# Two chained cross attentions on one core: memsets on VectorE, added attention, output sums and first FFN sums at other steps, and another order of the first attention's head groups

## The chip, the cores and the metric

The kernel runs on one core of one Trainium2 chip. The metric is the device time of one execution in microseconds. Engines are named as the profile does: PE is TensorE (matmuls and transposes), PEld its weight loads, DVE is VectorE, ACT is ScalarE, POOL is GpSimd, SP is SyncE, which here only issues DMAs.

## The reference

`x` and `ctx` have 32 items of 256 tokens by 256 features, all in float32. Two layers follow each other.

```python
# L0: 16 heads of 16 features
q, k, v = x @ Wq.T, ctx @ Wk.T, ctx @ Wv.T
att = softmax(q k^T / sqrt(16)) v
x = x + att[0]                     # item 0's attention is added to every item

# L1
nX = layernorm(ctx) * n1w + n1b
nF = layernorm(x) * n2w + n2b
attended = softmax(nF nX^T / 16) nX
h = gelu(attended @ fc1.T + fc1_b)             # 256 -> 4
cross = h @ fc2.T + fc2_b                      # 4 -> 256
nC = layernorm(cross) * n3w + n3b
self = softmax(nC nC^T / 16) nC
out = nF + gamma2 * (cross + gamma1 * self)
```

Since only `att[0]` is used, L0 is computed for item 0 alone. Since `h` has 4 columns, everything behind the first attention of L1 is done with rows of 5 or 6 numbers per token.

## The kernel before, in words

`x` stays in SBUF as `x_all` (128 partitions, 32 items, 2 halves of the tokens, 256 features). `ctx` comes in quarters of four items (`cq`). Every engine runs its instructions in the order in which the program issues them; nothing is reordered, so the order of the Python calls is the schedule.

**L0 (about 5 to 35 us).** The 16 heads are four groups (the fours) `j = 0..3`. For each, `head_queries(j)` makes the scores by queries (`sq`), `head_maxima` takes the negated maxima on VectorE (L493), `head_less(j)` turns them on TensorE (`pm`) and adds them into `qmT` on VectorE (L505), `head_keys(j)` makes the scores by keys (`sk`) and their exponentials on ScalarE (L514), `head_values(j)` multiplies them with the values (`ph`) and copies the result (L375, on ScalarE or VectorE), `head_turned(j)` turns it (`pt_h`), and its `weighted()` divides by the sums on VectorE (L534, L535). In between stand other works: `stats(n)` takes the statistics of items of `ctx` (VectorE, L211, two instructions an item), `moments_c` and `moments_ahead` make mean and scale of them (GpSimd, one power of some 1.65 us among them, L227), `even_normed` and `odd_normed` normalise token halves on GpSimd and ScalarE, and `setup_bias()` makes a row by a small product `p_b1f` with an addition on VectorE (L589). The PSUM banks of tag `tp` are two, and shared by nearly all of these.

**Cross attention (about 36 to 174 us).** `first_step(s)` runs for s = 0 to 34; scores exist for s = 0 to 31. In a step TensorE turns the exponentials of item s - 2 (`pt_e`), `x` of item s + 1 (`pt_x`), `ctx` of item s + 4 (`pt_c`), then multiplies the scores of item s (`sc`, L786). Each quarter has two more products (`pf` at b == 1, `pv` at b == 2, where b = s % 4). VectorE takes statistics of item s + 12 of `ctx` and s + 8 of `x` (L211), copies `pt_c` to `nxT` (L352), then takes the negated maximum `nm` of the scores (L796). ScalarE copies `pt_x` to `nfT` with a scale and a bias (L768) and makes the exponentials `e` (L799). GpSimd normalises `x` (L333) and `ctx` (L307), and at the end of a quarter makes the moments of the next one (`moments_both`, with a power of 2.93 us on 16 columns).

Works that belong to no single item are put at steps by hand:

- `add_attention(lo, hi)` (L758) is a DMA issued from GpSimd that adds `att` to items of `x_all` in SBUF. It must land before `stats_x` of these items.
- `zeroed`, eight memsets (L927) of the tiles `v_sl`, `u_sl`, `t_sl` at steps 8 to 15: six of 128x1024, then two of 128x64 and 128x128.
- The tables `between` (calls inside a step, just ahead of its scores) and `beside` (calls after the step). `hide(0, 4)` divides the first half of the FFN's inputs and adds the bias (a reciprocal, a product and a sum on VectorE, L1000, L1006, L1008). `activate(0)` is the gelu of them on ScalarE, with a table load (L1009). `third_a` to `third_d` are the third norm, by turns on GpSimd (`w_m`, `vgv`, `r` with a power, `w_k`) and VectorE.
- `output_gammas` and `output_bias` multiply and add rows of 5x256 on VectorE (L653, L654, L657, L658), `output_rows` does two more (L661, L662) and then issues eight small DMAs on SP's queue into `w_out`, which the output products read from 179 us on.

**Self attention and output (about 172 to 223 us).** An order written out word by word (`order`), TensorE always ahead.

Of the kernel before, what the change touches and what calls it, by code (L numbers as in the profile page):

```python
# [22 lines left out]
QB = 4  # L23
# [4 lines left out]
def tile_xattn_seq(  # L28
# [33 lines left out]
    nc = tc.nc  # L62
    B = x.shape[0]
    NQ = B // QB
    NT = B * NC
    TQ = QB * NC
    NM, NK = FH + 1, FH + 2
# [366 lines left out]
    def project_values(t, copy):  # L434
        pp = bank("tp", f"pp_v{t}")
        for dc in range(NC):
            nc.tensor.matmul(
                pp[:, t, :],
                c0T[:, dc, t * P : (t + 1) * P],
                wvT[:, dc, :],  # L440
                start=(dc == 0),
                stop=(dc == NC - 1),
            )
        copy(v1[:, t, :, 0:DK], pp[:, t, :].rearrange("p (h e) -> p h e", e=DK))
# [39 lines left out]
    def head_queries(j):  # L484

        sq = four_banks(f"sq{j}")
        qk = qT[:, j, :], kT[:, j, :]
        pair_products((0, *qk, sq[0:2]), (1, *qk, sq[2:4]))
        return sq

    def head_maxima(j, sq, heads):
        for i in heads:
            nc.vector.tensor_reduce(  # L493
                m_all[:, j % 2, :, i, ones_at[j % 2]], sq[i], AX.X, ALU.max, negate=True
            )
# [11 lines left out]
    def head_keys(j):  # L507

        sk = four_banks(f"sk{j}")
        kq = kT[:, j, :], qmT[:, j % 2, :]  # L510
        pair_products((0, *kq, sk[0:2]), (1, *kq, sk[2:4]))
        eT_of[j] = wk.tile([P, QB, NC, D], F32, tag="eTq", name=f"eT_h{j}", bufs=2)
        for i in range(QB):
            nc.scalar.activation(eT_of[j][:, i], sk[i], AF.Exp)  # L514
# [4 lines left out]
    def head_values(j, copy=nc.scalar.copy, by_pairs=False):  # L519
        col_of[j] = by_columns(  # L520
            tp_bank,
            f"h{j}",
            lambda kt, i: v1[:, kt, head_of(j, i), :],
            eT_of.pop(j),
            copy,
            by_pairs,
        )
# [55 lines left out]
    def setup_bias():  # L583
        pb = bank("tp", "p_b1f")
        for dc in range(NC):
            nc.tensor.matmul(
                pb[:, 0, 0:FH], ones, b1f[:, dc, :], start=(dc == 0), stop=(dc == NC - 1)
            )
        nc.vector.tensor_add(fc1b_all, pb[:, 0, 0:FH], fc1b_bc)  # L589
# [59 lines left out]
    w_out = const.tile([P, D], F32)  # L649
    nc.gpsimd.memset(w_out, 0.0)  # L650

    def output_gammas():
        nc.vector.tensor_mul(g1r, g1r, g2r)  # L653
        nc.vector.tensor_mul(g2r, g2r, m5)  # L654

    def output_bias():
        nc.vector.tensor_mul(tail, tail, g1r)  # L657
        nc.vector.tensor_add(g2r, g2r, tail)  # L658

    def output_rows():  # L660
        nc.vector.tensor_add(g2r, g2r, bias2)  # L661
        nc.vector.tensor_mul(g1r, g1r, k6[0:NM, :])  # L662
        for j in range(QB):
            nc.sync.dma_start(w_out[SL * j : SL * j + NM, :], g2r)
            nc.sync.dma_start(w_out[SL * j + NM : SL * j + 2 * NM, :], g1r)
# [6 lines left out]
    def stats(*ns):  # L672
        for n in ns:
            stats_c(n)
# [22 lines left out]
    head_less(1)()  # L697
    setup_outer()
    stats(3)
    project_values(1, on_scalar)  # L700
    moments_c(0)
    even_normed(0, 1, 2, 3)
    sq = head_queries(2)
    stats(4)
    head_maxima(2, sq, (0, 1))
    head_values(0)
    setup_bias()
    head_maxima(2, sq, (2, 3))
    head_keys(1)
    odd_normed(0, 1)  # L710
    weighted = head_turned(0)
    stats(5)
    head_less(2)()
    weighted()
    sq = head_queries(3)
    stats(6)
    head_maxima(3, sq, range(QB))
    head_values(1)
    odd_normed(2, 3)
    head_keys(2)  # L720
    weighted = head_turned(1)
    stats(7)
    moments_c(1)
    even_normed(4, 5)
    head_less(3)()
    weighted()
    head_keys(3)
    stats(8, 9, 10)
    head_values(2, by_vector)
    stats(11)  # L730
    odd_normed(4)
    head_values(3, on_scalar, True)
    c_ends = moments_ahead(2)
    weighted = head_turned(2), head_turned(3)
    for f in weighted:
# [140 lines left out]
    def first_step(s, between=()):  # L876
        q, b = s // QB, s % QB
        if b == 0 and 2 <= q and q + 4 < NQ:
            load_c(q + 4)
            if q == 2:  # L880
                load_x((NQ - 2) * QB, B)
        if s == QB:
            add_attention(QB * QB, (QB + 1) * QB)
        elif b == 0 and 1 < q < NQ - 3:
            add_attention((q + 3) * QB, (q + 4) * QB)

        late_turn = s in (27, 29, 31)
        if 0 <= s - 2 < B and not late_turn:
            cross_turned(s - 2)
        if 2 <= s < 2 * QB:  # L890
            for n in (2 * s, 2 * s + 1):
                stats_x(n)
            if s < QB:
                ends = first_moments(2 * s, 2 * s + 2)
        if QB <= s and s + 3 * QB < B:
            stats_c(s + 3 * QB)
        if s >= 2 * QB and s + 2 * QB < B:
            stats_x(s + 2 * QB)
        if b == QB - 1 and 4 <= q + 2 < NQ:
            if q + 3 < NQ:  # L900
                moments_both(q + 2)
            else:
                moments_x(q + 2, 0, QB)
        if QB < s < B - 1:
            turn_x(s + 1)
        for n in {9: (12,), 10: (13, 14), 11: (15,)}.get(s, ()):
            even_x(n)
        if 3 * QB <= s < B - 2 * QB:
            even_x(s + QB)

        for n in {10: (12, 13), 11: (14, 15), 12: (), 13: (16, 17), 16: (), 17: (20, 21)}.get(
            s, (s + QB,) if 3 * QB <= s < B - 2 * QB else ()
        ):
            odd_x(n)
        if B - 2 * QB < s <= B - QB:
            norm_x(s + QB - 1)
        if s + QB < B and s >= QB:
            turn_c(s + QB, on_scalar if s < QB + 2 else by_vector)
        for n in {7: (13,), 8: (14, 15), 9: (16, 17), 10: (18,)}.get(s, ()):
            norm_c(n)  # L920
        if 2 * QB + 2 < s < B - 2 * QB:
            norm_c(s + 2 * QB)
        for n, at in enumerate(scaled_at):
            if s == at:
                scale_skip(n)
        if 2 * QB <= s < 2 * QB + len(zeroed):
            nc.gpsimd.memset(*zeroed[s - 2 * QB])  # L927
        if b == 2 and 1 < q < NQ:
            values_turned(q)
        if b == 1 and 1 < q < NQ:  # L930
            values(q)
        if b == 2 and 0 < q <= NQ:
            cross_values(q - 1)
        if b == 3 and 0 < q <= NQ:
            cross_weighted(q - 1)
        for f, *args in between:
            f(*args)
        if s < B:
            softmax = cross_scores(s)
            if s <= QB:  # L940
                turn_x(s + 1)
            if s == 0:
                turn_c(6, nc.scalar.copy)
            softmax()
        if late_turn:
            cross_turned(s - 2, by_vector if s == B - 1 else on_scalar)
        if 1 <= s <= QB:
            stats_c(s + 3 * QB - 1)
        if s == 0:
            first_ends.pop()()  # L950
            add_attention(3 * QB, 4 * QB)
            add_first(3)
            first_ends.append(first_moments(3, QB))
            odd_normed(7)
        elif s == 1:
            first_ends.pop()()
            odd_normed(8)
            even_normed(8, 9)
        elif s == 2:
            ends()  # L960
            turn_c(7)
            load_c(5)
            odd_normed(9)
            even_normed(10)
        elif s == 3:
            ends()
            values(1)
            even_normed(11)
        elif s == QB:
            values_turned(1)  # L970
        if s in (QB, QB + 1):
            odd_normed(s + 6)
        if s == QB:
            moments_x(2, 0, 2)
        elif s == QB + 1:
            norm_x(2 * QB)
            moments_x(2, 2, QB)
        elif s == QB + 2:
            norm_x(2 * QB + 1)
            moments_c(3)  # L980
            norm_x(2 * QB + 2)
            norm_c(3 * QB)
        elif s == QB + 3:
            norm_x(2 * QB + 3)
        elif s == 2 * QB:
            moments_both(3)
# [179 lines left out]
    def activate(lo):  # L1166
        gelu_of.pop(lo)()

    between = {
        20: [(hide, 0, 4)],  # L1170
        28: [(turn_t, 0, by_vector)],
        29: [(turn_u, 2, by_vector), (early_weights, 0), (hide, 4, 6)],
        30: [(activate, 4), (third_a, 2), (turn_t, 1, by_vector)],
        31: [(third_c, 2), (self_values, 0)],
    }
    beside = {
        20: [(activate, 0), (third_a, 0)],
        21: [(third_b, 0), (third_a, 1)],
        22: [(third_c, 0), (third_b, 1)],
        23: [(output_gammas,), (output_bias,)],  # L1180
        24: [(third_d, 0), (output_rows,)],
        25: [(third_c, 1), (turn_u, 0, by_vector)],
        26: [(turn_u, 1, by_vector), (early_scores, 0), (third_d, 1)],
        28: [(early_scores, 1)],
# [197 lines left out]
```

## Time and profile before

| | us |
|---|---|
| time, median of 3 runs (226.4 to 227.15) | 226.84 |
| the profiled execution's own time | 226.24 |
| its span in the profile | 224.5 |
| TensorE busy in the span | 207.7 |
| VectorE busy | 170.2 |
| ScalarE busy | 146.5 |
| GpSimd busy | 174.3 |
| granted TensorE clock, mean | 0.989 |

The profile is of one execution. Its span runs from the first to the last instruction; the execution's own time is 1.7 us more. In a timeline row stand the start, the duration, the engine, the line, the operation, the tiles written and read, their shapes, how many instructions were merged, and in brackets the idle time of the engine before it with what ended it. Matmuls overlap, so a row's duration is longer than the distance to the next row; a pause of TensorE is seen in the starts. The step of a row is found by counting the scores: those of steps 8 to 16 start at 71.19, 75.32, 79.78, 83.14, 86.43, 90.56, 95.44, 98.80 and 101.84 us, those of steps 20 to 25 at 117.38, 122.13, 127.55, 130.91, 133.95 and 139.06.

### The profile page before, as it was taken

How to read it: one execution, taken by the hardware profiler on the slowest of the kernel's cores; microseconds unless marked ns; L12 is line 12 of the kernel's file. 1: busy time of each engine (PE TensorE's matmuls, PEld its weight loads, DVE VectorE, ACT ScalarE, POOL GpSimd, SP SyncE). 2: the span in 40 equal slices, each digit the busy share in tenths (PEclk: the TensorE clock that was granted, in tenths of full speed). 3: DMA queues.
4: the chain of work that ended last, by engine and by line, in shares of the span. 5: the costliest groups of instructions: out<-in, count | busy, mean ns of one | idle time of the engine just before them, and what ended most of it. 6: DMA issues, size and time to landing. Idle time of an engine off the chain costs nothing.

```text
span 224.5 us, 4955 instructions
## 1 busy us (share of the span) xinstructions
PE 207.7 (93%) x1797; PEld 152.7 (68%) x1797; DVE 170.2 (76%) x408; ACT 146.5 (65%) x300; POOL 174.3 (78%) x276
## 2 busy tenths in 40 slices
PE   7999988899999999999999898999999999999960
PEld 6666547576777888697796696787757566665640
DVE  2787989899988777758668579486548699978791
ACT  2454877698979488766766986548594684545510
POOL 6056588586889999999999889999229978999700
PEclk9999999999999999999999999999999999999995
DMA  7699998999976995082280000000000031542787
GB/s 212 218 334 352 391 385 226 177 260 244 247 131 242 306 200 189 1 141 49 38 153 0 1 3 1 6 3 0 3 1 0 3 142 48 219 158 93 274 311 262
DMA packets 18054, 33.81 MB, mean 151 GB/s; under 512 B 1191, under 2 KB 2158, under 8 KB 18030
## 3 DMA queue, kind: packets, MB, share of 16 engines
q1 hardware_dynamic: 12990, 24.33, 30.2%
q0 software_dynamic: 3696, 7.34, 18.9%
q10 hardware_dynamic: 1344, 1.84, 2.4%
q8 instruction: 14, 0.23, 0.4%
q14 instruction: 10, 0.08, 0.1%
HBM read 17.73 MB, written 8.39 MB: 116 GB/s over the span
## 4 chain that ended last, share of the span: by engine, by line
PE 43%; POOL 23%; DVE 16%; DMA 8%; ACT 4%; issue 3%; DVEq 0%; ACTq 0%; SPq 0%; POOLq 0%
PE sc L786 7%; POOL cq L307 6%; DVE st L211 5%; PE o L452 4%; DMA x_all<-att 4%; POOL rs_b L227 4%; PE k L452 4%; PE pu L364 4%; PE q L452 2%; PE sc L452 2%; POOL x_all L333 2%; DMA wk_nat<-in_L_xattn_Wk_dram 2%; DVE nm L796 2%; DMA fc_nat<-in_L_xattn_fc_w_dram 2%; PE ph L364 2%
## 5 line engine op out<-in xcount | busy, mean ns | idle before, releaser
L786 PE MATMUL sc<-nxT,nfT 128*128 128x256 f32 x256 | 62.4, 386 | 0.7 <-ACT nfT L768 0.7
L786 PEld LDWEIGHTS sc<-nxT,nfT 128*128 128x128 f32 x256 | 45.7, 190 | 12.1 <-issue 5.3
L799 ACT ACTIVATE e<-sc,nm 128x256 f32<-128x256 f32 x64 | 26.9, 472 | 26.1 <-DVE nm L796 25.8
L777 POOL TENSOR_TENSOR x_all<-x_all,w_bc 128x512 f32<-128x512 f32 x32 | 39.8, 1270 | 0.0
L796 DVE TENSOR_REDUCE nm<-sc 128x2 f32<-128x512 f32 x32 | 22.0, 688 | 23.2 <-PE sc L786 11.0
L768 ACT ACTIVATE nfT<-pt_x,bq,wq 128x256 f32<-128x256 f32 x64 | 33.2, 579 | 1.6 <-PE pt_x L202 1.5
L211 DVE BATCH_NORM_STATS2 st<-x_all 128x6 f32<-128x256 f32 x64 | 23.2, 412 | 2.6 <-DMA x_all<-att 2.5
L202 PE MATMUL pt_x<-ident,x_all 128*128 128x128 f32 x132 | 20.6, 277 | 2.9 <-POOL x_all L333 1.1
L202 PE MATMUL pt_c<-ident,cq 128*128 128x128 f32 x132 | 19.6, 275 | 1.4 <-ACT nfT L768 1.0
L211 DVE BATCH_NORM_STATS2 st<-cq 128x6 f32<-128x256 f32 x56 | 20.6, 412 | 0.0
L1225 DVE TENSOR_TENSOR x_all<-o,x_all 128x1024 f32<-128x1024 f32 (+1 forms) x19 | 18.1, 993 | 2.9 <-PE o L452 2.4
L1220 ACT ACTIVATE eT<-k 128x512 f32<-128x512 f32 (+1 forms) x19 | 14.3, 798 | 9.1 <-PE k L452 7.8
L202 PEld LDWEIGHTS pt_x<-ident,x_all 128*128 128x128 f32 x132 | 15.0, 141 | 6.9 <-POOL x_all L333 2.7
L307 POOL TENSOR_SCALAR cq<-cq,rs_b,nmr_b 128x256 f32<-128x256 f32 x32 | 19.4, 677 | 0.0
L202 PE MATMUL pt_e<-ident,e 128*128 128x128 f32 x128 | 19.1, 274 | 0.0
L808 ACT COPY eTq<-pt_e 128x512 f32<-128x512 f32 x31 | 17.9, 584 | 0.2 <-PE pt_e L202 0.2
L202 PEld LDWEIGHTS pt_e<-ident,e 128*128 128x128 f32 x128 | 15.6, 141 | 3.0 <-issue 0.4
L202 PEld LDWEIGHTS pt_c<-ident,cq 128*128 128x128 f32 x132 | 15.1, 141 | 2.6 <-ACT nfT L768 1.4
L352 DVE COPY nxT<-pt_c 128x512 f32<-128x512 f32 x23 | 15.5, 675 | 0.7 <-PE pt_c L202 0.7
L452 PE MATMUL o<-w_out,vt 32*128 32x256 f32 x128 | 13.3, 400 | 0.6 <-ACT vt L1101 0.5
L452 PE MATMUL k<-tt,ut 32*128 32x256 f32 x112 | 13.6, 397 | 0.0
L1207 DVE TENSOR_REDUCE t_sl<-q 128x4 f32<-128x1024 f32 (+1 forms) x12 | 12.3, 1041 | 0.3 <-PE q L452 0.2
(224 smaller groups left out, 433.3 us busy)
## 6 DMA issues: line engine op xcount, KB each, us to landing
out_dram<-x_all SPq DMA_DIRECT2D x15, 512.0 KB
x_all<-att POOLq DMA_DIRECT2D x7, 1024.0 KB, 9.2
cq<-in_ctx_dram SPq DMA_DIRECT2D x6, 1024.0 KB
x_all<-in_x_dram SPq DMA_DIRECT2D x4, 1024.0 KB
x_all<-in_x_dram SPq DMA_DIRECT2D x1, 2048.0 KB
x_all<-in_x_dram SPq DMA_DIRECT2D x1, 1792.0 KB
cq<-in_ctx_dram ACTq DMA_DIRECT2D x1, 1024.0 KB
cq<-in_ctx_dram SPq DMA_DIRECT2D x1, 768.0 KB
```

Of the source, the lines that this page charges most:

```text
L202: nc.tensor.transpose(pt[:, dc, t * P : (t + 1) * P], src[:, t, dc * P : (dc + 1) * P], ident)
L211: nc.vector.bn_stats(st[:, t, :], src[:, t, :])
L307: nc.gpsimd.tensor_scalar(row, row, rs[:, i + t, :], nmr[:, i + t, :], ALU.mult, ALU.add)
L352: copy(nxT_of[q][:, b], pt)
L452: nc.tensor.matmul(dst[i][:, t, :], lhs[r : r + SL, t * P : (t + 1) * P], rhs[r : r + SL, :], start=True, stop=True,)
L768: nc.scalar.activation(nfT_of[n][:, dc, :], px[:, dc, :], AF.Identity, bias=bq[:, dc : dc + 1], scale=wq2[:, dc : dc + 1],)
L777: nc.gpsimd.tensor_mul(x_all[:, n], x_all[:, n], w2_bc.unsqueeze(1).to_broadcast([P, NC, D]))
L786: nc.tensor.matmul(sc[:, qt, :], nfT[:, dc, qt * P : (qt + 1) * P], nxT[:, dc, :], start=(dc == 0), stop=(dc == NC - 1),)
L796: nc.vector.tensor_reduce(nm, sc, AX.X, ALU.max, negate=True)
L799: nc.scalar.activation(e[:, qt, :], sc[:, qt, :], AF.Exp, bias=nm[:, qt : qt + 1])
L808: copy(eT_of[q][:, b], turned(e_of.pop(n), "et", f"e_{n}"))
L1225: nc.vector.tensor_add(xs, po, xs)
```

## The change

In L0, the order of the calls after `stats(3)` is another one: `setup_bias`, the third group's queries and `stats(4)` come first, the four maxima of the third group stand together, the first group's values follow the second group's keys, the first group's weighting follows the last `head_less`, and the second group's `head_turned` follows the last keys. The third group's copy (L375) moves from VectorE to ScalarE. The added attention of items 24 to 27 goes from step 12 to step 11, that of items 28 to 31 from step 16 to step 15. The eight memsets go from GpSimd to VectorE, behind the maximum of their step. `hide(0, 4)` goes from the inside of step 20 to the end of step 19. The six output sums, in steps 23 and 24 before, are put one by one at the ends of steps 16, 17, 18, 21, 22 and 23, and the eight small DMAs follow the last one.

```diff
-    def output_gammas():
-        nc.vector.tensor_mul(g1r, g1r, g2r)
-        nc.vector.tensor_mul(g2r, g2r, m5)
-
-    def output_bias():
-        nc.vector.tensor_mul(tail, tail, g1r)
-        nc.vector.tensor_add(g2r, g2r, tail)
+    output_sums = [
+        lambda: nc.vector.tensor_mul(g1r, g1r, g2r),
+        lambda: nc.vector.tensor_mul(g2r, g2r, m5),
+        lambda: nc.vector.tensor_mul(tail, tail, g1r),
+        lambda: nc.vector.tensor_add(g2r, g2r, tail),
+        lambda: nc.vector.tensor_add(g2r, g2r, bias2),
+        lambda: nc.vector.tensor_mul(g1r, g1r, k6[0:NM, :]),
+    ]
 
     def output_rows():
-        nc.vector.tensor_add(g2r, g2r, bias2)
-        nc.vector.tensor_mul(g1r, g1r, k6[0:NM, :])
         for j in range(QB):
...
     stats(3)
+    setup_bias()
+    sq = head_queries(2)
+    stats(4)
     project_values(1, on_scalar)
     moments_c(0)
     even_normed(0, 1, 2, 3)
-    sq = head_queries(2)
-    stats(4)
-    head_maxima(2, sq, (0, 1))
+    head_maxima(2, sq, range(QB))
+    head_keys(1)
+    head_less(2)()
     head_values(0)
-    setup_bias()
-    head_maxima(2, sq, (2, 3))
-    head_keys(1)
+    stats(5, 6)
+    sq = head_queries(3)
     odd_normed(0, 1)
     weighted = head_turned(0)
-    stats(5)
-    head_less(2)()
-    weighted()
-    sq = head_queries(3)
-    stats(6)
     head_maxima(3, sq, range(QB))
     head_values(1)
     odd_normed(2, 3)
     head_keys(2)
-    weighted = head_turned(1)
+    head_less(3)()
     stats(7)
     moments_c(1)
     even_normed(4, 5)
-    head_less(3)()
     weighted()
     head_keys(3)
+    weighted = head_turned(1)
+    weighted()
+    head_values(2)
     stats(8, 9, 10)
-    head_values(2, by_vector)
+    head_values(3, on_scalar, True)
     stats(11)
     odd_normed(4)
-    head_values(3, on_scalar, True)
     c_ends = moments_ahead(2)
...
         if s == QB:
             add_attention(QB * QB, (QB + 1) * QB)
-        elif b == 0 and 1 < q < NQ - 3:
-            add_attention((q + 3) * QB, (q + 4) * QB)
+        elif s == 2 * QB:
+            add_attention((QB + 1) * QB, (QB + 2) * QB)
+        elif b == QB - 1 and 1 < q < QB:
+            add_attention((q + 4) * QB, (q + 5) * QB)
...
-        if 2 * QB <= s < 2 * QB + len(zeroed):
-            nc.gpsimd.memset(*zeroed[s - 2 * QB])
...
             softmax()
+        if 2 * QB <= s < 2 * QB + len(zeroed):
+            nc.vector.memset(*zeroed[s - 2 * QB])
...
     between = {
-        20: [(hide, 0, 4)],
...
     beside = {
+        16: [(output_sums[0],)],
+        17: [(output_sums[1],)],
+        18: [(output_sums[2],)],
+        19: [(hide, 0, 4)],
         20: [(activate, 0), (third_a, 0)],
-        21: [(third_b, 0), (third_a, 1)],
-        22: [(third_c, 0), (third_b, 1)],
-        23: [(output_gammas,), (output_bias,)],
-        24: [(third_d, 0), (output_rows,)],
+        21: [(third_b, 0), (third_a, 1), (output_sums[3],)],
+        22: [(third_c, 0), (third_b, 1), (output_sums[4],)],
+        23: [(output_sums[5],), (output_rows,)],
+        24: [(third_d, 0)],
```

## The prediction

> **What bounds the kernel now.** I read the page first, then TensorE's timeline through the cross attention, then the timelines of VectorE and GpSimd around each place where TensorE paused. On the page TensorE is busy nearly throughout, and GpSimd is full in slices 14 to 24 of the 40.
>
> ```profile
> PE 207.7 (93%) x1797; PEld 152.7 (68%) x1797; DVE 170.2 (76%) x408; ACT 146.5 (65%) x300; POOL 174.3 (78%) x276
> POOL 6056588586889999999999889999229978999700
> ```
>
> A busy share hides short pauses, so I measured TensorE's cadence in its timeline. Four transposes are followed by the next group 0.43 to 0.44 us later (88.16 to 88.59). Anything beyond that is a wait. The pairs below show five of them:
>
> ```profile
> 88.16 0.60 PE L202 MATMUL pt_e<-ident,e 128*128 128x128 f32 x4
> 88.59 0.60 PE L202 MATMUL pt_x<-ident,x_all 128*128 128x128 f32 x4
> 92.39 0.60 PE L202 MATMUL pt_e<-ident,e 128*128 128x128 f32 x4
> 93.20 0.66 PE L202 MATMUL pt_x<-ident,x_all 128*128 128x128 f32 x4 [0.21 <-POOL x_all L333]
> ...
> 103.57 0.60 PE L202 MATMUL pt_e<-ident,e 128*128 128x128 f32 x4
> 104.54 0.63 PE L202 MATMUL pt_x<-ident,x_all 128*128 128x128 f32 x4 [0.36 <-DVE nxT L352]
> ...
> 119.11 0.60 PE L202 MATMUL pt_e<-ident,e 128*128 128x128 f32 x4
> 120.13 0.63 PE L202 MATMUL pt_x<-ident,x_all 128*128 128x128 f32 x4 [0.42 <-DVE nxT L352]
> ...
> 125.75 0.66 PE L202 MATMUL pt_c<-ident,cq 128*128 128x128 f32 x4 [0.75 <-ACT nfT L768]
> ...
> 137.06 0.63 PE L202 MATMUL pt_x<-ident,x_all 128*128 128x128 f32 x4 [0.78 <-POOL sq_x L224]
> ```
>
> Start minus start minus 0.44 gives 0.37, 0.53, 0.58, then 0.92 at 125.75 (the group before began at 124.40) and 0.95 at 137.06 (before: 135.68). A sixth, 0.19, stands at 85.50. Together: 3.54 us. VectorE shows why for three of them:
>
> ```profile
> 103.05 0.75 DVE L211 BATCH_NORM_STATS2 st<-x_all 128x6 f32<-128x256 f32 x2 [0.91 <-DMA x_all<-att]
> 103.72 0.68 DVE L352 COPY nxT<-pt_c 128x512 f32<-128x512 f32 x1
> ...
> 118.64 0.75 DVE L211 BATCH_NORM_STATS2 st<-x_all 128x6 f32<-128x256 f32 x2 [1.62 <-DMA x_all<-att]
> ...
> 134.87 1.44 DVE L658 TENSOR_TENSOR g2r<-g2r,tail 5x256 f32<-5x256 f32 x1
> 136.24 0.67 DVE L352 COPY nxT<-pt_c 128x512 f32<-128x512 f32 x1
> ```
>
> TensorE's next x transposes start 0.15 behind the end of the copy nxT (104.40 to 104.54), and that copy stood behind statistics that waited for an added attention, or (at 137.06, whatever name the row gives) behind the output sums. GpSimd shows where the late transfers were issued:
>
> ```profile
> 94.16 0.95 POOL L927 MEMSET u_sl<- 128x1024 f32 x1
> 95.06 1.27 POOL L758 DMA_DIRECT2D x_all<-att  x1
> ...
> 134.64 1.40 POOL L1023 TENSOR_TENSOR w_k<-u_sl,gram_k 128x576 f32<-128x576 f32 x1
> ```
>
> **Added attention for items 24 to 31.** Issued in steps 11 and 15, no longer 12 and 16. In GpSimd's queue step 11 begins at 87.91 and step 15 at 102.65, against issues at 95.06 and 109.31. So both leave about 7 us sooner, and the 8 to 9 us to landing (95.06 to 103.0) then end before steps 16 and 20 read them. Each issue, 0.90 to the next start, now stands ahead of the combined moments of its step (4.7 us) and the norms behind them; the memsets gone from the same queue pay for that. x of 24 to 31 must have landed: its queue moved its last bytes by 82, GpSimd comes at about 85. Gain 0.53 + 0.58.
>
> **Memsets.** GpSimd loses six of about 0.92 and two small ones, 5.7 us. The pauses at 85.50 and 93.20 waited for its norms, which then come 1.8 and over 2 us sooner: gain 0.19 + 0.37. Further removal earns nothing there: the moments of steps 11 and 15 will wait for VectorE's statistics. VectorE gains the memsets, behind each step's maximum. Its one memset, 128x256, took 0.27, so 128x1024 is 1.08 by size. Behind the maximum (2.0 us after the scores start, 0.61 long) come memset M, two pairs of statistics (0.66 each) and the copy nxT (0.67), so the copy ends 4.60 + M after the scores of step s, and TensorE wants it, less the 0.15, 2.17 after the scores of step s + 1. There is room for M = period - 2.58. Periods by the score starts, pauses taken out: 4.13, 4.46, 3.36, 3.10, 4.13, 4.51 for steps 8 to 13, so the room is 1.55, 1.88, 0.78, 0.52, 1.55, 1.93. Step 10 then costs 0.30. Step 11 costs 0.56 less that 0.30, since its period grows by it. Sum 0.55. Bounds: nothing if M is 0.6 or less (an overhead inside the 0.27), 1.3 if each memset is held by one GpSimd norm (0.55) and M is 1.6. I take 0.55, the value by the only memset row. The two small ones (64 and 128 elements) fit into 0.78 and 0.46.
>
> **Output sums.** Four sums in step 23 took from 133.51 to 136.24; now one or none in a step, six steps in all, and the copy nxT of step 24 is on time: gain 0.95. Each costs 0.40 where nothing holds it. L658 took 1.44 beside GpSimd's w_k (134.64 to 136.04), so a sum can be held by a GpSimd operation. In steps 16 to 18 these are norms of 0.55, so a sum is 0.40 to 0.95 against room of 1.58, 1.88 and 0.78: at most 0.17, I take nothing. In steps 21 and 22 the room is over 1.4 beside 0.5 and 0.6 of other reductions; nothing, at most 0.3. The eight small transfers to w_out go out a step earlier on SP's queue, which at 138 has nothing behind it until 181; nothing.
>
> The Trainium skill, page SBUF — State Buffer, section SBUF: two separate sides, makes such holding general: a VectorE operation with two SBUF inputs and a GpSimd operation that reads SBUF exclude each other for the whole instruction. L658 agrees; L653 does not: it took its plain 0.40 at 133.51, inside the 2.93 us of GpSimd's power at 130.96.
>
> **FFN's first sums.** Reciprocal, product and sum (1.24 us with gaps) leave step 20, where they and the wait delayed the maximum to 121.13 (3.75 behind the scores' start at 117.38, normally 2.0), and stand behind step 19's maximum. Step 20 has no c statistics, so the copy is due at 3.94 + 1.24 + 0.15 = 5.3 against 3.04 + 2.17 = 5.2: cost 0.1. ScalarE's table load (1.28) and gelu follow the exponentials of step 20 and end some 5.2 behind the scores, before it was 6.9; the nfT behind them ends at 6.6, and TensorE wants it at 6.74 (4.13 + 2.61). So the 0.92 goes, with a margin of 0.1: gain 0.5 to 0.92, I take 0.92.
>
> **L0's fours.** I placed the new order by hand on each engine with the durations of the rows: products 1.07, values 1.00, bias product 0.54, four maxima 2.38, statistics 0.66, four exponentials 1.93. The bias product takes the place at 18.03. The third queries start at 18.57 (before 19.09), their maxima end at 22.11 (23.08, they were split by the bias's sum), the fourth maxima at 27.09 (27.64), the last exponentials at 31.3 (32.0), the last values at 32.4 (33.2). That is 0.7 to 0.8 sooner on TensorE and ScalarE. But VectorE idles 0.6 at 22.11 and 27.09 (for the turned maxima) and at 29.1 (for the second turned values, now behind the last keys), and the statistics of 8 to 11 (2.62) move behind that. They end at 32.7 (32.14), moments at 33.6, two weightings (1.07) at 34.7; before, the first added attention began at 34.78. From there to 60 the chain of waits runs mainly on VectorE, which the change leaves alone. Gain 0.1, bounds -0.7 to +0.6.
>
> **Sum.** 0.53 + 0.58 + 0.19 + 0.37 + 0.95 + 0.92 + 0.1 = 3.64, less 0.55 and 0.1: 3.0 us. Behind 137 the pauses that stay (0.45 at 142.65, where GpSimd is no releaser) hang on TensorE's own position, so the gain reaches the end. GpSimd's norm of item 27 ends at 140.43 and would be wanted at 140.81: just in time. The profiled execution took 226.24 us (span 224.5 and 1.7 around it), 0.6 under the median of 226.84; the changed one's profile should be 223.2, its median 223.8.
>
> **Rivals.**
> - L0 loses: VectorE's later statistics push the first added attention to 35.5. For it: VectorE is 8.8 to 9.7 of 10 us busy from 30 to 60. Against: the hand placement has it level. Price 0.8 more, and another 0.4 if the gelu's margin of 0.1 fails: 225.0. Chance 0.17.
> - GpSimd's power holds the FFN's sums, as w_k held L658: in step 19 the power (2.93) runs from about 2.4 to 5.3 behind the scores, the two sums with two inputs would end at 6.2, the copy at 7.5, and TensorE would lose 2.4. Time 226.2, within 0.3%. L653 speaks against. With other ways of ending level: chance 0.06. The Trainium skill's page SBUF — State Buffer, taken at its word, asks for this.
> - Slower: VectorE becomes the bound in steps 8 to 13. If each memset excludes GpSimd, as L658 and w_k did, and waits behind a power or two norms, M is 2.6: room is exceeded in steps 8 to 13 by 1.05 + 0 + 1.8 + 0.3 + 0.8 + 0, some 3.9, against the 3.55 of all gains, and GpSimd, held for 6 x 1.1 in its turn, keeps its two pauses of 0.56: 226.84 - 3.55 + 3.9 + 0.56 = 227.8. This decides from M of about 2.3. Against: the row of 0.27 ran while GpSimd's own memset did, and neither was stretched. Chance 0.10.
> - The forecast, 0.67.
>
> **Numbers.** About 0.3% (0.7 us) is what a measurement can tell here. Faster by more: forecast and first rival, 0.84; same 0.06; slower 0.10. The forecast's own range runs from 222.4 (M free, L0's 0.6) to 224.9; with the first rival 225.8.
>
> **What would show it.** Pauses at steps 11 to 25 gone but for some 0.3 before the x transposes of steps 12 and 13; no statistics waiting for an added attention behind 90; VectorE memsets near 1.08; L658's successor at 0.4 to 1.0; gelu ending 5.2 behind the scores of step 20; the first added attention at 34.7. Memsets over 2 us, or a copy nxT that TensorE awaits in each step, would prove me wrong.

## The result, and the profile after

The changed kernel takes 223.61 us (median of 5 runs, 223.31 to 223.96) against 226.40 for the kernel before in the same series (225.78 to 227.15): ratio 0.988, 95% interval 0.986 to 0.990. Its profiled execution took 223.84 us, span 222.1 (before 226.24 and 224.5): 2.4 us less, where the prediction's sum was 3.0.

The page after, rows of section 1 and 2 (busy time of each engine, GpSimd in 40 slices):

```profile
PE 206.9 (93%) x1797; PEld 153.3 (69%) x1797; DVE 174.0 (78%) x415; ACT 146.6 (66%) x301; POOL 169.0 (76%) x268
POOL 6047668676899999989929989999239978999700
```

VectorE has 3.8 us more, GpSimd 5.3 less, and GpSimd is still full in the middle: neither number says what was won. That is read from TensorE's timeline, at the places where it had paused (start, duration, then the operation; the idle time in brackets):

```profile
88.41 0.60 PE L202 MATMUL pt_e<-ident,e 128*128 128x128 f32 x4
89.06 0.63 PE L202 MATMUL pt_x<-ident,x_all 128*128 128x128 f32 x4
89.67 0.66 PE L202 MATMUL pt_c<-ident,cq 128*128 128x128 f32 x4
...
103.83 0.60 PE L202 MATMUL pt_e<-ident,e 128*128 128x128 f32 x4
104.27 0.60 PE L202 MATMUL pt_x<-ident,x_all 128*128 128x128 f32 x4
...
124.35 0.66 PE L202 MATMUL pt_c<-ident,cq 128*128 128x128 f32 x4 [0.26 <-ACT nfT L765]
```

At 103.83 the transposes follow each other by 0.44 again, and so they do at 93.08, 118.82 and 134.28. New are 0.21 at 89.06 and 0.17 at 89.67, and 0.42 of the 0.92 stay at 124.35.

Since starts of a run differ by up to half a microsecond, the kernels are compared by periods: the start of the scores of one step less that of the step before. Only these differ between before and after by more than 0.03 (us):

| from step | before | after | what it is |
|---|---|---|---|
| 0 | 3.91 | 4.09 | L0's order, reaching into the first steps |
| 11 | 3.29 | 3.04 | norm on GpSimd, pause at 85.50 |
| 12 | 4.13 | 4.57 | memsets on VectorE |
| 13 | 4.88 | 4.45 | norm on GpSimd, pause at 93.20 |
| 16, 20 | 4.69, 4.74 | 4.13, 4.13 | added attention |
| 21 | 5.42 | 4.94 | the FFN's first sums and gelu |
| 24 | 5.11 | 4.13 | output sums |

Steps 0 to 31 take 2.69 less, L0 gives back another 0.25, and from step 31 to the end both take 55.5: what was won before 140 us reaches the end whole, as the prediction had it.

VectorE after, the maximum, the memset, statistics and the copy of step 11, then the two-input operations of `hide` and one output sum:

```profile
86.01 0.68 DVE L793 TENSOR_REDUCE nm<-sc 128x2 f32<-128x512 f32 x1
86.85 0.91 DVE L943 MEMSET u_sl<- 128x1024 f32 x1 [0.16 <-issue]
87.68 0.69 DVE L211 BATCH_NORM_STATS2 st<-cq 128x6 f32<-128x256 f32 x2
...
88.94 0.67 DVE L352 COPY nxT<-pt_c 128x512 f32<-128x512 f32 x1
...
117.03 0.29 DVE L1005 TENSOR_TENSOR pre<-n_all,rd_f 128x128 f32<-128x128 f32 x1
117.36 0.29 DVE L1007 TENSOR_TENSOR pre<-pre,fc1b_all 128x128 f32<-128x128 f32 x1
...
124.67 0.82 DVE L656 TENSOR_TENSOR g2r<-g2r,tail 5x256 f32<-5x256 f32 x1
```

From 86.01 to 87.68 are 1.67. Before, without a memset, the statistics of the same step followed 0.61 behind the maximum:

```profile
85.12 0.69 DVE L796 TENSOR_REDUCE nm<-sc 128x2 f32<-128x512 f32 x1 [0.56 <-ACT nfT L768]
85.73 0.74 DVE L211 BATCH_NORM_STATS2 st<-cq 128x6 f32<-128x256 f32 x2
```

So a memset costs VectorE some 1.07 (the row is 0.91, with 0.16 idle ahead of it).

GpSimd after (the added attention of items 24 to 27, the moments of step 19 and their power):

```profile
85.73 1.16 POOL L755 DMA_DIRECT2D x_all<-att  x1
...
115.20 0.24 POOL L222 TENSOR_TENSOR df_b<-st 128x16 f32<-128x16 f32 x1 [3.71 <-DVE st L211]
...
116.50 2.92 POOL L227 TENSOR_TENSOR rs_b<-ve_b,neg_half 128x16 f32<-128x16 f32 x1
```

The two transfers go out at 85.73 and 98.02, 9.3 and 11.3 us sooner than before, and no statistics behind 90 wait for one.

### The profile page after: what moved, and what is told of

It is laid out like the page before. It is cut to its first block, busy times and chain, and to the rows that moved or that the text cites. A ratio compares the mean times of both kernels' runs of the same rounds, so it can differ in the third digit from the quotient of the medians.

```text
span 222.1 us, 4964 instructions
## 1 busy us (share of the span) xinstructions
PE 206.9 (93%) x1797; PEld 153.3 (69%) x1797; DVE 174.0 (78%) x415; ACT 146.6 (66%) x301; POOL 169.0 (76%) x268
## 4 chain that ended last, share of the span: by engine, by line
PE 63%; DVE 12%; POOL 7%; ACT 4%; issue 2%; DVEq 0%; POOLq 0%; ACTq 0%
PE sc L783 20%; PE pt_e L202 5%; PE o L452 5%; PE pt_c L202 4%; PE pt_x L202 4%; PE k L452 4%; DVE st L211 4%; PE pu L364 4%; PE pv L364 3%; PE q L452 2%; PE sc L452 2%; PE pf L364 2%; POOL rs_c L227 2%; DVE nm L793 2%; DVE x_all L1227 2%
## 5 line engine op out<-in xcount | busy, mean ns | idle before, releaser
L211 DVE BATCH_NORM_STATS2 st<-cq 128x6 f32<-128x256 f32 x56 | 19.9, 403 | 0.0
L202 PEld LDWEIGHTS pt_x<-ident,x_all 128*128 128x128 f32 x132 | 15.5, 143 | 5.2 <-POOL x_all L333 1.8
L307 POOL TENSOR_SCALAR cq<-cq,rs_b,nmr_b 128x256 f32<-128x256 f32 x32 | 17.9, 574 | 0.0
```

The lines of the kernel that those rows point to most:

```text
L202: nc.tensor.transpose(pt[:, dc, t * P : (t + 1) * P], src[:, t, dc * P : (dc + 1) * P], ident)
L211: nc.vector.bn_stats(st[:, t, :], src[:, t, :])
L307: nc.gpsimd.tensor_scalar(row, row, rs[:, i + t, :], nmr[:, i + t, :], ALU.mult, ALU.add)
```

## The experiments

Each ran beside the kernel before, whose medians were 226.2 to 226.5 in these series. "Before plus" is the kernel before with one part of the change; "after with" is the changed kernel with one edit.

**Before plus the memsets on VectorE.** `nc.gpsimd.memset` inside the step becomes `nc.vector.memset` behind `softmax()`.

> The kernel before with the eight memsets on VectorE alone; the added attentions keep steps 12 and 16. Theory one (a memset of 1.07 on VectorE is free where the step's period leaves room, period less 2.58): the pauses at 85.50 and 93.20 go, one of 0.4 comes ahead of the scores of step 13. GpSimd's queue is 3.7 us shorter by step 12, so the added attention of items 24 to 27 is issued near 91.5 and lands near 99.5, ahead of step 16: the pauses at 104.54 and 120.13 go too. In all 0.6 + 1.1 - 0.4 = 1.3 us faster, 225.1. Theory two (added attention is late only because of the step at which it stands): those two pauses stay, and the gain is 0.2 or less, 226.2.

Measured 223.79 us, ratio 0.990 (0.988 to 0.991). This one part brings nearly all of the change, and more than the 1.3 us that were expected of it. Periods: 11 at 3.04, 12 at 4.57, 13 at 4.45, as in the whole change; but also 16 and 20 at 4.13 and 21 at 4.58; the 0.84 that period 21 loses was not expected. GpSimd, free of 5.7 us, reaches the unmoved added attention sooner (before: 95.06 and 109.31):

```profile
91.92 1.27 POOL L758 DMA_DIRECT2D x_all<-att  x1
106.10 1.27 POOL L758 DMA_DIRECT2D x_all<-att  x1
```

Three microseconds are enough for both transfers to land in time. So the prediction's 0.53 + 0.58 belongs as much to the memsets as to the move.

**Before plus the added attention's move.**

```diff
-        elif b == 0 and 1 < q < NQ - 3:
-            add_attention((q + 3) * QB, (q + 4) * QB)
+        elif s == 2 * QB:
+            add_attention((QB + 1) * QB, (QB + 2) * QB)
+        elif b == QB - 1 and 1 < q < QB:
+            add_attention((q + 4) * QB, (q + 5) * QB)
```

> The kernel before with the added attention of items 24 to 31 in steps 11 and 15 alone. Theory one: the pauses at 104.54 and 120.13 go (1.1 us), but GpSimd still carries the memsets and has the issue (0.90) ahead of the norm that TensorE awaited at 93.20, so that pause grows from 0.4 to about 1.3. With the maximum of step 20 on time the gelu's pause shrinks from 0.9 to 0.4 or less. Gain 0.7 to 1.1: 225.1 to 225.5 beside 226.2. Theory two (the issue's own time on GpSimd costs nothing): 93.20 stays at 0.4, gain 1.6 or more, 224.6.

Measured 225.30, ratio 0.995 (0.994 to 0.997). The pauses of periods 16 and 20 go, and 0.84 of period 21, but period 13 rises from 4.88 to 6.06. TensorE and GpSimd there:

```profile
94.13 0.66 PE L202 MATMUL pt_x<-ident,x_all 128*128 128x128 f32 x4 [1.38 <-POOL x_all L333]
```

```profile
87.64 1.16 POOL L758 DMA_DIRECT2D x_all<-att  x1
...
93.52 0.56 POOL L333 TENSOR_SCALAR x_all<-x_all,rs_b,nmr_b 128x256 f32<-128x256 f32 x1
```

With the memsets still in the queue the issue stands ahead of the moments, and the norm of 93.52 comes that much later; TensorE's transposes begin 0.05 behind the norm's end (94.08). In the whole change the emptied queue pays for it, as the prediction said of the issue's price.

**Before plus the output sums at single steps.** The tables `between` and `beside` of the change, for the six sums and the rows only.

> The kernel before with the six output sums alone at steps 16, 17, 18, 21, 22 and 23. Theory one (L658 beside GpSimd's w_k made TensorE wait at 137.06): that pause of 0.95 is gone and the others stay, so the scores of step 25 come 0.9 to 1.0 us sooner: 225.4 to 225.5 beside 226.4. Theory two (GpSimd, which the profile names as the releaser, held TensorE): the pause stays, no difference.

Measured 225.43, ratio 0.996 (0.995 to 0.998). Period 24 falls from 5.11 to 4.13, 0.98. Period 16 rose by 0.40 in the profiled run: its transfer to items 24 to 27 landed 8.4 us after its issue instead of 8.0, while TensorE stood 0.4 earlier. A pause that waits for a transfer takes up what comes ahead of it.

**Before plus `hide` at step 19.**

```diff
     between = {
-        20: [(hide, 0, 4)],
...
     beside = {
+        19: [(hide, 0, 4)],
```

> The kernel before with the FFN's first sums at the end of step 19 alone. Theory one (they delayed the maximum of step 20, and through the exponentials the table load and the gelu): they now run while VectorE waits for the added attention, the maximum of step 20 comes 1.2 us sooner and the pause of 0.9 at 125.75 goes: 225.3 beside 226.2. Theory two (the added attention alone sets that maximum and the gelu): the pause stays, no difference.

Measured 225.13, ratio 0.995 (0.993 to 0.996). Period 21 falls from 5.42 to 4.45, all of its pause, and period 20 stays at 4.72, held by the transfer. So the place of `hide` costs nothing by itself, and it alone can bring the whole of the gelu's gain; in the change only 0.48 arrives.

**L0 alone: before plus the new order, and after with the old order.**

> The kernel before with L0's new order alone. Theory one (VectorE is last in the new order, since the statistics of items 8 to 11 stand behind the second weighting): the first added attention starts at 35.2 instead of 34.8, the scores of steps 1 to 8 come 0.4 to 0.5 us later, and the whole is 0.3 to 0.5 us slower, about 226.8 to 226.9 beside 226.4. Theory two (the 0.5 us at step 1 of the changed kernel came from another part): the first added attention at 34.8 and no difference.

> The changed kernel with L0's old order put back, all else kept. Theory one: the scores of steps 1 to 8 start at the times of the kernel before, and the 0.5 us that the new order lost is gained whole: 223.1 beside the changed kernel's 223.6, ratio to before some 0.9855. Theory two: the fours' earlier maxima and exponentials help later steps, and the time is that of the changed kernel or longer.

Before plus the new order: 226.56 against 226.19, ratio 1.002 (1.001 to 1.003). After with the old order: 223.23, ratio 0.9875 (0.986 to 0.989); that is 0.38 under the changed kernel's median, but of another series, and the ratio can't be told from the changed kernel's 0.9877. The traces of the two kernels agree with the first comparison: from `qmT` of the second group to the first added attention the new order takes 17.58 instead of 17.24, and to the scores of step 1 0.41 to 0.44 more. So it costs 0.4. VectorE after, at two of its three waits (the first, 0.59, ends at 22.93), then the late statistics and the first added attention:

```profile
28.06 0.42 DVE L505 TENSOR_TENSOR qmT<-pm,qT 128x256 f32<-128x256 f32 x1 [0.65 <-ACT cq L322]
...
30.26 0.21 DVE L534 RECIPROCAL rd_h<-pt_h 128x8 f32<-128x8 f32 x1 [0.69 <-PE pt_h L382]
...
30.71 2.70 DVE L211 BATCH_NORM_STATS2 st<-cq 128x6 f32<-128x256 f32 x8
...
35.20 0.69 DVE L832 TENSOR_TENSOR x_all<-x_all,att 128x512 f32<-128x512 f32 x1
```

Before, the third and fourth additions into `qmT` came without such a wait:

```profile
23.82 0.42 DVE L505 TENSOR_TENSOR qmT<-pm,qT 128x256 f32<-128x256 f32 x1
...
28.41 0.42 DVE L505 TENSOR_TENSOR qmT<-pm,qT 128x256 f32<-128x256 f32 x1
```

The three waits of 0.6 to 0.7 are the ones of the hand placement, but they end at 22.9, 28.1 and 30.3 where it had 22.7, 27.7 and 29.7 (22.11, 27.09 and 29.1 with 0.6 each), and the statistics end at 33.4 instead of 32.7.

**After with statistics put into these waits.** In L0's new order, `stats(5)` stands between the call of `head_less(2)` and its second half, `stats(8)` likewise at `head_less(3)`, `stats(9, 10)` ahead of the second weighting; `stats(7)`, `moments_c(1)` and `even_normed(4, 5)` come ahead of the fourth group's queries.

> The changed kernel with L0's new order kept on TensorE, but the statistics of items 5, 6, 7, 8, 9 and 10 put where VectorE idles in it: ahead of the third and fourth sums into qmT and ahead of the second weighting. Theory one (VectorE is last in the new order because it idles 0.6 at each of three places and does the statistics afterwards): from the second sum into qmT to the first added attention 16.9 us instead of 17.6 (old order 17.2), and 0.5 to 0.7 us faster than the changed kernel. Theory two (the chain through the turned maxima sets the end): 17.5 or more, no gain.

Measured 223.39, ratio 0.987 (0.984 to 0.989), within the spread of the changed kernel. Period 0 is 3.90 again and the first added attention comes 17.28 behind `qmT`, 0.30 sooner; 16.9, and 0.5 to 0.7 us in all, were expected. Of the three waits one stays, shortened to 0.39, and VectorE gets a longer one, for the last values:

```profile
33.37 0.21 DVE L534 RECIPROCAL rd_h<-pt_h 128x8 f32<-128x8 f32 x1 [1.24 <-PE pt_h L382]
```

So the waits were the loss, and nearly without them the new order is level with the old one (17.24), not better: behind VectorE stands TensorE's last group of values.

**After with ScalarE's norm of item 24 one step later.** In the changed kernel the gelu of step 20 comes like this on ScalarE:

```profile
119.95 0.60 ACT L338 ACTIVATE x_all<-x_all,nmr_b,rs_b 128x256 f32<-128x256 f32 x1 [0.94 <-POOL nmr_b L236]
120.46 0.82 ACT L796 ACTIVATE e<-sc,nm 128x256 f32<-128x256 f32 x2
...
122.59 0.31 ACT L1008 ACTIVATE v_sl<-pre 128x128 f32<-128x128 f32 x1
```

The maximum of step 20 ended at 119.78 (119.09 + 0.69), but ahead of the exponentials in the queue stands the norm of item 24, which waits for GpSimd's moments until 119.95. Before, the same exponentials had waited for the maximum:

```profile
121.84 0.84 ACT L799 ACTIVATE e<-sc,nm 128x256 f32<-128x256 f32 x2 [1.25 <-DVE nm L796]
```
 The edit moves the norm behind the gelu:

```diff
-        for n in {10: (12, 13), 11: (14, 15), 12: (), 13: (16, 17), 16: (), 17: (20, 21)}.get(
+        for n in {10: (12, 13), 11: (14, 15), 12: (), 13: (16, 17), 16: (), 17: (20, 21), 20: (), 21: (24, 25)}.get(
```

> The changed kernel with ScalarE's norm of item 24 in step 21, behind nfT, instead of step 20. Theory one (in step 20 ScalarE waited 0.94 for the moments that GpSimd ended at 119.9, and with it the exponentials, the table load, the gelu and nfT): the remaining pause of 0.42 ahead of the scores of step 22 goes: 0.4 us faster than the changed kernel, ratio to before 0.986 or less. Theory two (the gelu and its table loads alone make nfT late, and the norm only moves behind them): the pause stays or a new one of the same size comes in step 23.

Measured 223.02, ratio 0.985 (0.983 to 0.987). The interval still touches the changed kernel's, but the trace is clear: period 21 is 4.45, the pause is gone. ScalarE there, with the scores of step 20 at 117.02:

```profile
121.89 0.31 ACT L1008 ACTIVATE v_sl<-pre 128x128 f32<-128x128 f32 x1
...
122.58 1.02 ACT L765 ACTIVATE nfT<-pt_x,bq,wq 128x256 f32<-128x256 f32 x2
```

The gelu ends 5.18 behind the scores (122.20 less 117.02), the figure that the prediction gave for the change itself, where it is 5.81.

**After with the third output sum in step 17.** The moments that this norm waits for begin 0.1 behind the statistics of step 18, and these stand behind the sum at 113.40.

```diff
-        17: [(output_sums[1],)],
-        18: [(output_sums[2],)],
+        17: [(output_sums[1],), (output_sums[2],)],
```

> The changed kernel with the third output sum (g1r times tail) in step 17 beside the second, no longer in step 18. In the changed kernel the period from step 21 to 22 is 4.94 us where hide alone, attention alone or the memsets alone brought it to 4.45 to 4.58; GpSimd's moments for the norm that ScalarE's step-20 exponentials stand behind begin at 115.20, 0.10 behind the statistics of step 18, which stand behind this sum (0.40 at 113.40). Theory (the sum delays the statistics, these the moments, these ScalarE's norm, table load and gelu): moments 0.33 to 0.40 sooner, period 21 to 22 down to 4.55 to 4.6, time 223.2 to 223.3. Rival (the hide's own work in step 19 holds the gelu back): period stays at 4.94, 223.6.

Measured 223.50, ratio 0.987 (0.985 to 0.989). The median can't tell it from the changed kernel, the trace can: the moments, 115.20 less 114.05 = 1.15 behind the scores of step 19 in the changed kernel, now stand 0.83 behind them (113.80):

```profile
114.63 0.24 POOL L222 TENSOR_TENSOR df_b<-st 128x16 f32<-128x16 f32 x1 [3.17 <-DVE st L211]
```

Period 21 falls from 4.94 to 4.60. So of the 0.49 that is missing there, 0.34 was lost by an output sum three steps earlier, over statistics, moments, norm, exponentials and gelu. With the norm moved in ScalarE's queue, as above, the whole 0.49 goes.

**After with the memsets in steps that have room.**

```diff
+    zeroed_at = [8, 9, 12, 13, 16, 17, 14, 18]
...
-        if 2 * QB <= s < 2 * QB + len(zeroed):
-            nc.vector.memset(*zeroed[s - 2 * QB])
+        if s in zeroed_at:
+            nc.vector.memset(*zeroed[zeroed_at.index(s)])
```

> The changed kernel with its six memsets of 128x1024 behind the maximum of steps 8, 9, 12, 13, 16, 17 (now 8 to 13) and the two small ones in steps 14 and 18 (now 14, 15). In the changed kernel the period of TensorE's scores from step 12 to step 13 grew from 4.13 to 4.57 us, the only place where the memsets cost anything, and the memsets of steps 10 and 11 stand where periods are 3.36 and 3.04. Theory (a memset costs only what exceeds its step's room, period less 2.58): steps 10 and 11 are free of them, the period 12 to 13 is 4.13 again, those behind 16 and 17 stay 4.13 and 4.45 (memset and output sum, 1.5 us, against a room of 1.55 and 1.88), and the time falls by 0.44 to 223.2. Rival (the cost comes from the memsets' sum on VectorE or from a wait of another operation that only shows at step 12): the 4.57 stays or the 0.44 comes back at 16 or 17, 223.6.

Measured 223.47, ratio 0.987 (0.985 to 0.989). Period 12 is 4.13 again, and 16 and 17 keep 4.13 and 4.45 with a memset and an output sum each; period 21 rises by 0.06, from 4.94 to 5.00. The transposes at the place of the first of the two new pauses, 0.43 apart:

```profile
88.16 0.60 PE L202 MATMUL pt_e<-ident,e 128*128 128x128 f32 x4
88.59 0.60 PE L202 MATMUL pt_x<-ident,x_all 128*128 128x128 f32 x4
```

So the whole price of the memsets, 0.44, comes from the two in steps 10 and 11. The median is 0.14 under the changed kernel's in another series, less than the 0.44 but within the intervals; the periods show the gain, the medians don't.

**After with every memset issued twice.**

```diff
+            nc.vector.memset(*zeroed[s - 2 * QB])
```

> The changed kernel with each of the eight memsets issued twice in a row, so that VectorE bears 2.1 us instead of 1.07 behind the maximum of steps 8 to 13. By the prediction's room rule (room is the period less 2.58: 1.55, 1.88, 0.78, 0.52, 1.55, 1.93; a step that costs lengthens the next step's period and room by as much): 0.6 at step 8, 0 at 9, 1.36 at 10, 0.26 at 11, 0.33 at 12, 0 at 13: 2.5 in all, where one memset was counted at 0.55 and cost 0.43. So 1.5 to 2.1 more than the changed kernel: 225.1 to 225.7. If memsets and GpSimd shut each other out (the slower rival), GpSimd's moments and norms of steps 8 to 13 stretch too, its pauses at steps 11 and 13 return, and the time passes 226.4. If VectorE's queue has slack that the rule doesn't count: 224.5 or less.

Measured 229.16, ratio 1.012 (1.010 to 1.014): 5.6 us more than the changed kernel, far beyond the 1.5 to 2.1 that the room rule gave. VectorE of that kernel, from the maximum of step 10 to that of step 11:

```profile
84.37 0.68 DVE L793 TENSOR_REDUCE nm<-sc 128x2 f32<-128x512 f32 x1
85.21 0.91 DVE L943 MEMSET u_sl<- 128x1024 f32 x1 [0.16 <-issue]
86.40 0.91 DVE L944 MEMSET u_sl<- 128x1024 f32 x1 [0.28 <-DVE u_sl L943]
...
89.19 0.68 DVE L793 TENSOR_REDUCE nm<-sc 128x2 f32<-128x512 f32 x1
```

From 79.23 to 104.08 us (the maxima of steps 9 and 14) VectorE has no gap but those at the memsets; its five steps take 24.85, where the changed kernel's periods 9 to 13 take 19.87. It has become the bound. The rule failed in one clause: "a step that costs lengthens the next step's period and room by as much". It does not, since the next maximum stands in VectorE's queue behind the late copy and starts late by as much. The lateness is handed on until a step has true slack. What counts is VectorE's work from maximum to maximum against the period, summed over neighbouring steps. GpSimd's rows show nothing of a mutual lock: its power takes 2.92 and 2.93 there and its pairs of `ctx` norms 1.09, as without the second memsets.

**The mended kernel: after with L0's old order, the roomier memsets and the later norm of item 24.**

> The changed kernel with three of its steps mended: L0's fours in the order of before (0.3 to 0.4 sooner by the runs with each order), the memsets in steps 8, 9, 12, 13, 16, 17, 14, 18 (0.44), and ScalarE's norm of item 24 one step later (step 21, period 21 to 22 4.45 instead of 4.94). If the three add, as places in different stages should: 223.5 less 0.35, 0.44 and 0.49, so 222.2 to 222.4, ratio to the kernel before near 0.982. If they overlap (a memset in step 16 or 17 delays the moments behind it, and the gelu's wait returns): 222.6 to 222.9.

Measured 222.33, ratio 0.982 (0.980 to 0.984), against 0.988 (0.986 to 0.990) for the changed kernel: the three mendings add, and beat both kernels. Its periods 0, 12 and 21 are 3.90, 4.13 and 4.45.

## Why the prediction was right, and where its steps were not

The time came out 0.2 under the forecast and inside the range, but the gain was smaller than forecast: 2.4 between the profiled executions and 2.8 between the medians, where the sum was 3.0. The forecast started from three runs of the kernel before, with a median of 226.84; with two more runs (225.99 and 225.78) the median is 226.40. So two errors of opposite sign met, and that the time itself came within 0.2 is in part luck. The terms, by the periods of the profiled executions:

| step of the prediction | predicted | measured |
|---|---|---|
| added attention | 0.53 + 0.58 | 0.56 + 0.61 |
| GpSimd's pauses at 85.50 and 93.20 | 0.19 + 0.37 | 0.25 + 0.43 |
| output sums | 0.95 | 0.98 |
| FFN's first sums, gelu | 0.92 | 0.48 |
| `hide` in step 19 | -0.10 | 0 |
| memsets on VectorE | -0.55 | -0.44 |
| L0's fours | +0.10 | -0.43 |
| sum | 3.0 | 2.4 |

*Added attention, GpSimd's pauses, output sums.* Sizes right within 0.06, read from the pauses. The cause of the first was told too narrowly: memsets alone or move alone end the wait, so the parts do not add (from step 0 to 31 the memsets alone win 2.29, the whole change 2.69). The move was not needed once the queue was empty. In the changed kernel the sums took 0.40 to 0.51, and 0.82 where GpSimd's norms ran (124.67), within the 0.4 to 1.0 given.

*FFN's first sums.* The mis-sized term. The chain, table load and gelu behind the exponentials of step 20, is right, and its 5.2 and 6.6 are what the kernel with the later norm shows (5.18, and nfT 6.58). Left out was what stands ahead of these exponentials in ScalarE's queue: the norm of item 24. Before, it was hidden, since the maximum came at 121.13; with the maximum early it became the last to arrive. The output sum in step 18 made it 0.32 later still, though "nothing" was put for that sum: it was weighed against the room of the copy nxT alone, not against the statistics that GpSimd's moments wait for. The margin of 0.1 was stated; it was overdrawn by 0.49.

*The rival that GpSimd's power holds the FFN's sums* fell: in the changed kernel the two took 0.29 each, at 117.03 and 117.36, inside the power of 116.50 to 119.42. By the Trainium skill, page SBUF — State Buffer, section SBUF: two separate sides, an operation of VectorE with two SBUF inputs and one of GpSimd that reads SBUF exclude each other for the whole instruction. The row of the power disagrees; that of L656 (0.82 beside norms of 0.55) agrees that such an operation can be held.

*Memsets.* The price per memset was right (1.08, measured 1.07) and the sum nearly (0.55, 0.44), by a rule that holds only near its own point. All of it showed in one period, not 0.30 and 0.26 in two: the transposes of `x` behind the scores of step 12 began 0.21 late, 0.10 behind the end of nfT (88.96), which stood in ScalarE's queue behind exponentials that had waited for the maximum of 86.01; the profile names no releaser for them, so this cause is read from the times alone. Those of `ctx` began another 0.17 late, 0.06 behind the end of the copy nxT (89.61). The slower rival had the right mechanism, VectorE the bound in steps 8 to 13, with a wrong point: it was to decide from M of about 2.3, by mutual exclusion and with GpSimd held too. At M of 2.26, without any exclusion, the kernel is already at 229.2, and a straight line between the two measured points (1.07 and 223.6, 2.26 and 229.2) puts the break-even at about 1.7. This estimate is on the low side, since with a smaller M fewer steps exceed their room. It is still close to the 1.6 that the prediction itself named as M's upper bound, so the 1.3 that it gave for that bound was probably too small; no run has that M.

*L0.* The sign was wrong, inside the stated bounds. The hand placement had the three waits of VectorE at the right operations; what was mis-sized is when they end (qmT at 22.93 and 28.06, the second weighting at 30.26, where 22.7, 27.7 and 29.7 were placed). The errors add up, because the statistics stand behind them all, and the first added attention came at 35.20, not at 34.7. The rival "L0 loses" priced 0.8 for it; 0.53 of that came (0.43 lost where 0.10 was to be won), together with the gelu's lost margin that it named as its second half, 0.49 for 0.4. Forecast and rival were no alternatives but two ends of one scale.

## What to carry to other kernels

Where an engine's queue is served in order, ask for every early result what stands ahead of its user: a norm that waits for another engine takes the place of the wait that was removed. Before parts of a change are added up, see which of them empty the same queue: the memsets alone had freed the transfers that another part moved by hand. Put new work where the period exceeds the engine's own work from mark to mark, and count lateness as handed on, not as repaid.

## What was not expected of the hardware

An operation of VectorE with two SBUF inputs ran unheld inside GpSimd's power (0.29 and 0.29 within 2.92), and was lengthened from 0.40 to 0.82 beside GpSimd's norms of `ctx`, whose pair took 1.26 instead of 1.10: not every GpSimd operation holds it. A second memset of the same tile starts 0.28 after the first ends, so each further one costs 1.19, not 1.07. The DMA of the added attention to items 24 to 27, issued from GpSimd, landed 7.9 to 8.6 us after its issue in the fourteen traces; the 0.4 between the kernel before (8.0) and the run with the output sums moved (8.4) is the 0.40 by which period 16 grew.
